# One load for both graphs of a pair, and a rewritten end, in a four-layer graph network on one core

## The chip, the cores and the metric

The kernel runs on one core of one Trainium2 chip. Such a core has TensorE (matrix products, called PE; its weight loads are listed apart as PEld), VectorE (DVE), ScalarE (ACT), GpSimd (POOL) and SyncE (SP, which here only issues transfers), and 16 DMA engines that move data between DRAM and the on-chip memories. The metric is the time of one execution on the device in microseconds. Before the change it is 1578.65 us, the median of three runs (1576.26 to 1581.45).

## The reference

There are 128 graphs of 64 nodes with 128 features each (`x`), and a weighted adjacency matrix of 64 by 64 per graph (`adj`), about a quarter of it nonzero. Four layers follow each other, each as `x = layernorm(x + layer(x, adj))`:

- Layers 0 and 1 compute a filter for every pair of nodes from its distance: Gaussians of the distance (20 in layer 0, 64 in layer 1), a matrix to 128 features, a shifted softplus, a second matrix. Layer 0 multiplies the filter by a cosine cutoff, layer 1 by the squared adjacency value. Node i then receives the sum over j of filter(i, j) times features(j), and two small matrices with a softplus between them finish the layer.
- Layer 2 is a graph convolution: elu twice after a first matrix, then two products with the normalised adjacency matrix, each after a matrix, with an elu between them.
- Layer 3 is one product with a normalised adjacency matrix, a matrix and a relu.

```python
    x = _layernorm(x + _L0_gnn_ref(x, adj, ...), axis=-1)
    x = _layernorm(x + _L1_gnn_ref(x, adj, adj, ...), axis=-1)
    x = _layernorm(x + _L2_gnn_ref(x, adj, ...), axis=-1)
    x = _layernorm(x + _L3_gnn_ref(x, adj, ...), axis=-1)
```

## The kernel before, in words

Nearly all work is in the edges of layers 0 and 1, and only the nonzero ones are computed. At the start the kernel sorts the graphs and the nodes by their numbers of edges, packs the nonzero distances, the numbers of their neighbours and their weights into lists of fixed length ("slots of edges"), and stores these lists in DRAM: `d` (distance, four bytes), `j` (neighbour, two bytes) and `w` (weight, four bytes). The length of a list, `GSLOTS`, is 948 to 1,092 in layer 0 and 1,140 to 1,260 in layer 1, and differs by set; there are eight sets of eight pairs. The packing of later sets runs beside the edge work of earlier ones, in layer 0.

The edge work goes over 128 slots: 64 pairs of graphs in layer 0, then the same 64 in layer 1. One graph of the pair lies on partitions 0 to 63 and the other on 64 to 127. The lists of a pair are copied to all partitions of their half: each row of `j` and `w`, and of `d` in layer 1, is the same list. In layer 0 a list of distances is cut into thirds, each copied to 20 rows (the last to 24), one row per Gaussian. `later_loads` (L1362 and on) issues these loads on SP's queue: `d` first, and `j` and `w` by the inner function `late`, some steps later. Before the change every load brings the rows of one graph, so that layer 1 takes six loads a slot and layer 0 ten. There are three buffers for `d` and `w` and two for `j`, so the loads of a slot are issued one to three slots ahead, once the buffer's last reader is done.

The slots are worked off two at a time, in four to six steps of some thousand edges per graph (`steps_of`). A step makes filters for its edges: `filter_in` (L1827, into PSUM `px`), two activations to `h` (exponential and logarithm), `filter_out` (L1842, `pw`), `gather` (L1856, `pg`: the neighbours' features by a product with a one-hot matrix), and `message` (L1882, DVE, product of both). `slot_sums` (L1912, L1916) adds the messages by node. ACT's `gaussians` squares and exponentiates `d`; DVE's `one_hot` (L1803) turns `j` and `w` into the weighted one-hot matrix, in place of `w`.

When a group of pairs has its sums, queues of generators follow, one small piece of each per step: `nodes` (`node_after`: the end of layers 0 and 1), `convs` (`graph_convs`: layers 2 and 3 of groups of four pairs, one queue for even and one for odd groups), and `last` for three small last groups of two, one and one pairs. `at_phase` holds a convolution back until a given step of a pair of slots. `layernorm` takes mean and variance on DVE; for groups of four pairs the root and the scaling run on GpSimd (L1460, L1461, L1466), for smaller groups on ACT and DVE. Each piece gets its PSUM from `bank`, two buffers for all of them. Results leave through `store_rows` (GpSimd, indirect) or, for the last small groups, a plain store on SP.

The order is written out: at the end `in_order` ties every instruction of an engine to the one before it on that engine, so each engine works in the order in which the program lists its instructions, and a wait holds up all that is behind it. After the last step the queues are drained in turns, one piece of each.

Of the kernel before, what the change touches and what calls it, by code (L numbers as in the profile page):

```python
# [12 lines left out]
F32 = mybir.dt.float32  # L13
# [6 lines left out]
P = 128  # L20
A = 64
# [591 lines left out]
def sparse_stack(ctx: ExitStack, tc: tile.TileContext, t: dict, out: bass.AP, flag):  # L613
# [122 lines left out]
    def dram_ap(ap, offset, dims):  # L736
        return bass.AP(tensor=ap.tensor, offset=ap.offset + offset, ap=dims)
# [118 lines left out]

    at_step = [0]

    def at_phase(k):
        while phase[0] not in (k, None):  # L860
            yield

    def steps_later(n):
        to = at_step[0] + n
        while at_step[0] < to:
            yield
# [498 lines left out]
    def later_loads(n):  # L1365


        layer, p = pair_at(n)
        s = p // 8
        size = GSLOTS[layer][s]  # L1370
        at = (p % 8) * 2 * size
        assert (layer, s) in stored, "slots are read before they are written"
        d = edge.tile([P, MAX_SLOTS], F32, tag="d", name=f"d_{n}", bufs=3)
        j = edge.tile([P, MAX_SLOTS], BF16, tag="j", name=f"j_{n}")
        w = edge.tile([P, MAX_SLOTS], F32, tag="w", name=f"w_{n}", bufs=3)

        def load(to, name, first, n):
            engine.dma_start(to, dram_ap(slots[layer, name][s], first, [[0, to.shape[0]], [1, n]]))  # L1378

        third = size // 3  # L1380
        d = d[:, 0 : size if layer else third]
        for b in range(2):
            rows, first = slice(A * b, A * (b + 1)), at + b * size
            engine = nc.sync
            if layer == 1:
                load(d[rows], "d", first, size)
            else:
                for k, end in enumerate((NG0, 2 * NG0, A)):
                    engine = nc.scalar if n == 0 and b * k == 0 else nc.sync
                    load(d[A * b + NG0 * k : A * b + end], "d", first + k * third, third)  # L1390

        def late():
            nonlocal engine
            engine = nc.sync
            for b in range(2):
                rows, first = slice(A * b, A * (b + 1)), at + b * size
                load(j[rows, 0:size], "j", first, size)
                load(w[rows, 0:size], "w", first, size)

        return (d, j, w), late  # L1400

# [19 lines left out]

    def bank(name, n=GS):
        ps = ps_n.tile([P, 512], F32, tag="n", name=name)[:, 0 : n * P]
        return ps, ps.rearrange("p (s c) -> p s c", s=n)

# [7 lines left out]
    def tiled(name, n, q):  # L1435


        tag = f"c{q % 2}" if n == GS else f"c_{q}"
        return rings[0].tile([P, n * P], F32, tag=tag, name=f"{name}_{q}", bufs=4)

# [7 lines left out]
    def layernorm(y, dst, n, name, quick=False):  # L1448

        stats = node.tile([P, GS, 6], F32, tag="st", name=f"st_{name}", bufs=4)[:, 0:n]  # L1450
        mv = node.tile([P, GS, 2], F32, tag="mv", name=f"mv_{name}", bufs=4)[:, 0:n]
        for s in range(n):
            nc.vector.bn_stats(stats[:, s, :], y[:, s, :])
            nc.vector.bn_aggr(mv[:, s, :], stats[:, s, :])  # L1454
            if s + 1 == GS // 2 < n and not quick:
                yield
        rstd = node.tile([P, GS], F32, tag="rs", name=f"rs_{name}", bufs=4)[:, 0:n]
        yield
        if n == GS:
            nc.gpsimd.tensor_scalar(rstd, mv[:, :, 1], LN_EPS, None, ALU.add)  # L1460
            nc.gpsimd.tensor_tensor(rstd, rstd, neg_half[:, 0:n], ALU.pow)  # L1461
        else:
            act(rstd, mv[:, :, 1], AF.Ln, bias=ln_eps)
            act(rstd, rstd, AF.Exp, scale=-0.5)
        for s in range(n):
            (nc.gpsimd if n == GS else nc.vector).tensor_scalar(  # L1466
                dst[:, s, :], y[:, s, :], mv[:, s, 0:1], rstd[:, s : s + 1],
                ALU.subtract, ALU.mult,
            )
        yield  # L1470
# [128 lines left out]
    def node_after(layer, q, agg):  # L1599


        w = layers[layer]
        name = f"{layer}_{q}"
        n = agg.shape[1]
        codes = node_codes.pop((layer, q))
        u, by = bank(f"u_{name}", n)
        share = by_pair(shares.pop(q)) if layer == 0 else None
        for s in range(n):
            of = agg[:, s, :]
            if n > 1:  # L1610
# [36 lines left out]
        yield from layernorm(y, xs, n, name, layer == 1)  # L1647
        if layer == 1:
            if n < GS:
                yield from graph_convs(q)  # L1650
            else:
                convs[q % 2].append(graph_convs(q))

    def elu(ps, bias, i, q, also=()):

# [40 lines left out]

        act(to, ps, AF.Copy)

    normals = {}

    def normals_of(q):

# [9 lines left out]
    def graph_convs(q):  # L1712
# [14 lines left out]
            return y  # L1727

        if n == GS:
            yield from at_phase(6)  # L1730
            scaled(2, q)
        flat, ps = bank(f"gx_{q}", n)
        for s in range(n):
# [17 lines left out]
        yield True  # L1751
        nT3 = by_pair(tiled("nTs3", n, q)) if n == GS else normals[3, q]
        h1 = yield from elu(flat, g["b1"], 1, q, normal(3, q, nT3) if n == GS else ())
        y2 = yield from times("hw2", lambda s: h1[:, s, :], lambda s: g["W2"])
        _, ps = bank(f"o2_{q}", n)
        for s in range(n):
# [4 lines left out]
        yield  # L1761
        yield from layernorm(z, xs, n, f"2_{q}")
        if n == GS:
            yield from at_phase(2)
        y3 = yield from times("sup", lambda s: xs[:, s, :], lambda s: nT3[:, s, :])
        flat, ps = bank(f"o3_{q}", n)
        nc.tensor.matmul(
# [153 lines left out]
            else:  # L1921
                nodes.append(node_after(layer, q, agg))

    befores, nodes, convs, sums = deque(), deque(), (deque(), deque()), deque()
    small_groups, small = range(NP // GS - 1, len(GROUPS[1])), {}
    at_end = range(NP // GS - 2, len(GROUPS[1]))
    last = {q: deque() for q in small_groups}
# [122 lines left out]
    for i in range(len(steps) + 2):  # L2050
# [29 lines left out]
        if c is not None:  # L2080
# [4 lines left out]
            for part_ in c["parts"]:  # L2085
# [25 lines left out]
        if layer == 0:  # L2111
            slot(nodes)
            if befores and phase[0] in BEFORES[beat]:
                slot(befores)
        if c2 is not None:
            filter_out(c2)
        for queue in last.values():
# [2 lines left out]
            slot(nodes)  # L2120
        if c2 is not None:
            message(c2)
        for _ in range(1 + (n >= N - MORE)):
            if convs[0]:
                slot(convs[0])
# [5 lines left out]
        for _ in range(1 + (n >= N - MORE)):  # L2131
            slot(convs[1])
        for queue in last.values():
            slot(queue)
        past = [c, c1]
    phase[0] = None
    run(sums, -1)
# [52 lines left out]
```

## Time and profile before

| | |
|---|---|
| median of three runs | 1578.65 us |
| profiled execution | 1577.26 us |
| its span | 1575.4 us |
| PE busy | 1427.4 us, 91% |
| DVE, ACT busy | 1316.5 us (84%), 1313.8 us (83%) |
| POOL busy | 759.3 us, 48% |
| mean DMA rate over the span | 131 GB/s |
| first and last `filter_in` of layer 0 | 67.6 and 725.2 us |
| first and last `filter_in` of layer 1 | 729.2 and 1494.7 us |
| last `one_hot` | 1481.7 us |

The profile is one execution taken by the hardware profiler; times in it count from the start of its span. A busy share is an average over the whole run and says little by itself: the stages have different limits, so the table of busy time by stage is read first, then the chain of waits (from the last instruction back, at each step to what released it), then the DMA queues, where a packet is one contiguous piece moved by one DMA engine, and a completion is a further packet of four bytes. A label such as L1842 is a line of the kernel before; L955 is a helper through which all activations go. The names left and right of an arrow are what an instruction writes and reads.

### The profile page before, as it was taken

The page shows a single profiled execution, that of the slowest core. Times are in us where ns is not written, and L with a number is a line of the kernel's source. Part 1 is how long each engine was busy: PE and PEld are TensorE (multiplying, and loading weights), DVE is VectorE, ACT ScalarE, POOL GpSimd, SP SyncE. Part 2 cuts the span into 40 slices and gives each one's busy share as a digit, 9 for nine tenths or more (in the row PEclk, how much of TensorE's full clock was granted, in tenths as well). Part 3 has the DMA queues.
Part 4 walks back from the last instruction along what each step waited for, and adds up shares of the span by engine and source line. Part 5 has one row for each costly group of instructions (what it writes and reads, how often), then busy time and mean ns, then how long its engine had stood idle before and what let it go on. Part 6 is the DMA issues. An engine that isn't in the chain of part 4 may idle for free.

```text
span 1575.4 us, 23201 instructions
## 1 busy us (share of the span) xinstructions
PE 1427.4 (91%) x6841; PEld 790.8 (50%) x6841; DVE 1316.5 (84%) x2895; ACT 1313.8 (83%) x1647; POOL 759.3 (48%) x1175
## 2 busy tenths in 40 slices
PE   1387999999989999999999999999999999998974
PEld 1143454554444445554444555555555655554553
DVE  8796988888989899788788888888888888878763
ACT  1366897989888989899999999999999999988742
POOL 2435256365564545333912334555544665555544
PEclk9999999999999999999999999999999999999985
DMA  6766454545555545447665655555555555654100
GB/s 205 258 139 137 101 136 116 129 123 136 130 142 124 141 130 135 125 114 167 155 152 142 143 132 132 147 133 136 139 130 138 139 132 131 150 132 106 31 7 23
DMA packets 122280, 205.60 MB, mean 131 GB/s; under 512 B 47956, under 2 KB 80034, under 8 KB 121506
## 3 DMA queue, kind: packets, MB, share of 16 engines
q1 hardware_dynamic: 113330, 188.40, 48.2%
q0 software_dynamic: 6576, 14.99, 2.9%
q8 instruction: 57, 0.93, 0.3%
q10 hardware_dynamic: 2240, 0.65, 0.2%
q14 instruction: 77, 0.63, 0.1%
HBM read 185.29 MB, written 18.64 MB: 129 GB/s over the span
## 4 chain that ended last, share of the span: by engine, by line
PE 61%; ACT 11%; DVE 9%; DMA 6%; issue 4%; SPq 2%; POOL 2%; another core or an unknown queue 1%; DVEq 0%; ACTq 0%; POOLq 0%
PE pw L1842 23%; PE px L1827 13%; PE pg L1856 11%; ACT h L955 5%; DVE m L1882 2%; DMA w<-w_dram 2%; DVE agg L1912 2%; DMA j<-j_dram 2%; ACT d L955 2%; PE y L1491 1%; PE hw L1722 1%; SPq L1378 1%; PE u L1615 1%; PE back L1641 1%; PE o L1632 1%
## 5 line engine op out<-in xcount | busy, mean ns | idle before, releaser
L955 ACT ACTIVATE h<-h,half 128x1008 f32<-128x1008 f32 (+12 forms) x313 | 332.8, 1063 | 0.1
L955 ACT ACTIVATE m<-pg 128x1008 f32<-128x1008 f32 (+12 forms) x313 | 291.8, 933 | 46.1 <-DVE agg L1916 21.0
L1856 PE MATMUL pg<-w,ys 64*128 64x504 f32 (+15 forms) x1376 | 299.4, 518 | 27.0 <-ACT d L955 7.5
L1842 PE MATMUL pw<-h,w_L_gnn_W2T 128*128 128x504 f32 (+8 forms) x640 | 300.2, 592 | 2.6 <-DVE m L1882 2.4
L1882 DVE SCALAR_TENSOR_TENSOR m<-pw,c_L_gnn_b,m 128x1008 f32<-128x1008 f32 (+8 forms) x161 | 194.8, 1211 | 113.6 <-PE pw L1842 97.7
L1912 DVE TENSOR_REDUCE agg<-m 128x32 f32<-128x544 f32 (+14 forms) x455 | 287.2, 669 | 1.8 <-PE u L1615 0.4
L1842 PE MATMUL pw<-h,w_L_gnn_fw 128*128 128x504 f32 (+6 forms) x608 | 253.6, 540 | 9.7 <-DVE m L1882 7.7
L1882 DVE SCALAR_TENSOR_TENSOR m<-pw,c_L_gnn_fb,m 128x1008 f32<-128x1008 f32 (+6 forms) x152 | 168.8, 1111 | 69.9 <-PE pw L1842 47.2
L955 ACT ACTIVATE h<-px,c_L_gnn_b 128x1008 f32<-128x1008 f32 (+8 forms) x160 | 171.4, 1071 | 30.2 <-PE px L1827 30.0
L955 ACT ACTIVATE h<-px,c_L_gnn_fb 128x1008 f32<-128x1008 f32 (+6 forms) x152 | 148.2, 975 | 53.8 <-PE px L1827 37.9
L1856 PEld LDWEIGHTS pg<-w,ys 64*128 64x128 f32 x1376 | 129.0, 189 | 118.6 <-issue 50.3
L1842 PEld LDWEIGHTS pw<-h,w_L_gnn_W2T 128*128 128x128 f32 x640 | 109.4, 191 | 153.5 <-issue 82.0
L1803 DVE SCALAR_TENSOR_TENSOR w<-j,row,w 128x1212 f32<-128x1212 bf16 (+12 forms) x128 | 181.3, 1416 | 5.4 <-DMA w<-w_dram 5.4
L1827 PE MATMUL px<-d,fw 64*128 64x168 f32 (+10 forms) x928 | 155.4, 440 | 27.1 <-DMA d<-d_dram 18.4
L1827 PE MATMUL px<-d,w1t 64*128 64x504 f32 (+11 forms) x768 | 173.1, 542 | 0.5 <-ACT h L955 0.4
L1460 POOL TENSOR_SCALAR rs<-mv 128x4 f32<-128x4 f32 x61 | 15.0, 245 | 288.7 <-DVE mv L1454 288.0
L1842 PEld LDWEIGHTS pw<-h,w_L_gnn_fw 128*128 128x128 f32 x608 | 105.3, 193 | 90.9 <-issue 44.9
L1827 PEld LDWEIGHTS px<-d,fw 64*128 64x128 f32 x928 | 74.4, 189 | 127.8 <-issue 36.1
L955 ACT ACTIVATE d<-d,neg_off 128x1212 f32<-128x1212 f32 (+12 forms) x128 | 120.9, 945 | 8.2 <-DMA d<-d_dram 8.2
L995 POOL DMA_INDIRECT rows<-comb,goes x64 | 71.0, 1110 | 108.9 <-DMA rows<-comb,goes 64.5
L1466 POOL TENSOR_SCALAR x_all<-ny,mv,rs 128x128 f32<-128x128 f32 x124 | 109.2, 889 | 3.3
L995 POOL DMA_INDIRECT out_dram<-gz,at_row x56 | 75.1, 1341 | 60.1 <-DMA out_dram<-gz,at_row 55.0
(264 smaller groups left out, 2300.8 us busy)
## 6 DMA issues: line engine op xcount, KB each, us to landing
d<-d_dram SPq DMA_DIRECT2D x32, 315.0 KB
w<-w_dram SPq DMA_DIRECT2D x32, 315.0 KB
d<-d_dram SPq DMA_DIRECT2D x32, 303.0 KB
w<-w_dram SPq DMA_DIRECT2D x32, 303.0 KB
w<-w_dram SPq DMA_DIRECT2D x32, 252.0 KB
j<-j_dram SPq DMA_DIRECT2D x32, 157.5 KB
j<-j_dram SPq DMA_DIRECT2D x32, 151.5 KB
d<-d_dram SPq DMA_DIRECT2D x16, 300.0 KB
```

Of the source, the lines that this page charges most:

```text
L955: latest = nc.scalar.activation(out_, in_, func, **kw)
L995: nc.gpsimd.indirect_dma_start(out=into, out_offset=bass.IndirectOffsetOnAxis(ap=at, axis=0), in_=rows, in_offset=None,)
L1378: engine.dma_start(to, dram_ap(slots[layer, name][s], first, [[0, to.shape[0]], [1, n]]))
L1466: (nc.gpsimd if n == GS else nc.vector).tensor_scalar(dst[:, s, :], y[:, s, :], mv[:, s, 0:1], rstd[:, s : s + 1], ALU.subtract, ALU.mult,)
L1491: nc.tensor.matmul(ps[:, s, :], lhsT=xt[:, s * P : (s + 1) * P], rhs=w["win"], start=True, stop=True)
L1615: nc.tensor.matmul(by[:, s, :], lhsT=w["o1"], rhs=of, start=layer == 1, stop=True)
L1803: nc.vector.scalar_tensor_tensor(hots[n][:, 0:size], j[:, 0:size], near, wt[:, 0:size], ALU.is_equal, ALU.mult)
L1827: nc.tensor.matmul(ps[:, b, at : at + m], lhsT=w["w1"][rows, :] if c["layer"] else w["w1"][rows, k, :], rhs=d[rows, col : col + m], start= ...
L1842: nc.tensor.matmul(c["pw"][:, b, :], lhsT=c["w"]["w2"], rhs=c["h"][:, b, :], start=True, stop=True)
L1856: nc.tensor.matmul(ps[:, b, to], lhsT=y[rows, :], rhs=hots[part_["n"]][rows, first:stop], start=True, stop=True,)
L1882: nc.vector.scalar_tensor_tensor(to, c["pw"][:, :, of], c["w"]["b2"], to, ALU.add, ALU.mult)
L1912: nc.vector.tensor_reduce(av[:, :, :, r], both, AX.X, ALU.add)
```

## The change

Three things are changed.

The first is `later_loads`. One load now brings the rows of both graphs of a pair: the destination is all 128 partitions, and the source is read as [2][64][size], the first step going from one graph's list to the other's, the second repeating a list 64 times. In layer 0 two of the three thirds of one graph are brought by one load, [2][20][third].

```diff
-        def load(to, name, first, n):
-            engine.dma_start(to, dram_ap(slots[layer, name][s], first, [[0, to.shape[0]], [1, n]]))
+        both = [[size, 2], [0, A], [1, size]]
+
+        def load(to, name, first, dims):
+            engine.dma_start(to, dram_ap(slots[layer, name][s], first, dims))
...
-        for b in range(2):
-            rows, first = slice(A * b, A * (b + 1)), at + b * size
-            engine = nc.sync
-            if layer == 1:
-                load(d[rows], "d", first, size)
-            else:
-                for k, end in enumerate((NG0, 2 * NG0, A)):
-                    engine = nc.scalar if n == 0 and b * k == 0 else nc.sync
-                    load(d[A * b + NG0 * k : A * b + end], "d", first + k * third, third)
+        engine = nc.sync
+        if layer == 1:
+            load(d, "d", at, both)
+        else:
+            for b in range(2):
+                first = at + b * size
+                load(d[A * b : A * b + 2 * NG0], "d", first, [[third, 2], [0, NG0], [1, third]])
+                engine = nc.scalar if n == 0 and b == 0 else nc.sync
+                load(
+                    d[A * b + 2 * NG0 : A * (b + 1)], "d", first + 2 * third,
+                    [[0, A - 2 * NG0], [1, third]],
+                )
+                engine = nc.sync
 
         def late():
...
-            for b in range(2):
-                rows, first = slice(A * b, A * (b + 1)), at + b * size
-                load(j[rows, 0:size], "j", first, size)
-                load(w[rows, 0:size], "w", first, size)
+            load(j[:, 0:size], "j", at, both)
+            load(w[:, 0:size], "w", at, both)
```

The second is the end after the last step. Six queues (`x`, `y`, `z` for the small groups, `a`, `b`, `c` for the convolutions) get a PSUM bank of their own each, cut out of the banks of the edge work, and a written string says whose turn is next; a turn goes on until its queue has issued something.

```diff
     def bank(name, n=GS):
+        if own_banks:
+            ps = own_banks[now_run[0]][:, 0 : n * P]
+            return ps, ps.rearrange("p (s c) -> p s c", s=n)
...
-    while nodes or convs[0] or convs[1] or any(last.values()) or stores:
-        for queue in (*last.values(), nodes, *convs):
-            slot(queue)
+    run(nodes, -1)
+    for pool, tag, keys in ((ps_x, "x", "zy"), (ps_g, "g", "ab"), (ps_w, "w", "xc")):
+        both = pool.tile([P, 2, 512], F32, tag=tag, name=f"own_{tag}")
+        for h, key in enumerate(keys):
+            own_banks[key] = both[:, h, :]
+    queues = dict(zip("xyz", last.values()), n=nodes, a=convs[0], b=convs[1], c=convs[2])
+    turns = 'cbzyxybazyxzybcbcbaxyycybbczxyczxaxzyczxzxabxyczcbzyxcbybazxbxyczzcbzczycxyyyzyczcbyxczxzzbxxyzxzycbczcyxczcyyxzyzyzbxxyxzbzxczxzxzzcyyxczzyz'
+    while any(queues.values()):
+        for key in turns:
+            now_run[0], size = key, len(block)
+            while queues[key] and len(block) == size:
+                run(queues[key], 1)
+            run(stores, 1)
+        turns = "zyxcba"
```

The third is what leads up to it. After the last step, and for the three norms of the last group of four pairs (`LAST`, group 14), root and scaling run on ACT and DVE. This group gets a third convolution queue and tiles of its own; the small groups' normalised matrices (`normals_of`) are begun 14, 11 and 8 slots before the end; convolutions are free of their phase in the last four slots instead of eight, and wait one or two steps there; the sums of the last pair are shared out differently.

```diff
-        if n == GS:
+        apart = n == GS and not own_banks and name not in own_names
+        if apart:
             nc.gpsimd.tensor_scalar(rstd, mv[:, :, 1], LN_EPS, None, ALU.add)
             nc.gpsimd.tensor_tensor(rstd, rstd, neg_half[:, 0:n], ALU.pow)
...
-            (nc.gpsimd if n == GS else nc.vector).tensor_scalar(
+            (nc.gpsimd if apart else nc.vector).tensor_scalar(
...
-    def at_phase(k):
+    def at_phase(k, later=0):
+        if phase[0] is None and not own_banks:
+            yield from steps_later(later)
         while phase[0] not in (k, None):
             yield
...
-                convs[q % 2].append(graph_convs(q))
+                convs[2 if q == LAST else q % 2].append(graph_convs(q))
...
-            yield from at_phase(6)
+            while q == LAST and (3, q - 2) not in turned:
+                yield
+            yield from at_phase(6, 1)
...
-    FREE, MORE = 8, 0
+    FREE, MORE, ONCE, FAST = 4, 4, 1, (0, 0)
+    SUMS = (2, 2, 3, 4, 4)
+    EARLY = {N - gap: q for gap, q in zip((14, 11, 8), small_groups)}
...
-        if n >= N - 4:
-            run(sums, (2, 2, 5, 4, 2)[k] if c is not None else 9)
+        if n >= N - 2:
+            run(sums, SUMS[k] if c is not None else 9)
...
-                if layer == 1 and part_["s"] == 0 and q in last:
-                    last[q].append(normals_of(q))
+                if m in EARLY:
+                    last[EARLY[m]].append(normals_of(EARLY[m]))
```

More of the change, by code (lines that the diff above doesn't have):

```diff
@@ L1375, in later_loads @@
         w = edge.tile([P, MAX_SLOTS], F32, tag="w", name=f"w_{n}", bufs=3)
-        def load(to, name, first, n):
-            engine.dma_start(to, dram_ap(slots[layer, name][s], first, [[0, to.shape[0]], [1, n]]))
+        both = [[size, 2], [0, A], [1, size]]
+        def load(to, name, first, dims):
+            engine.dma_start(to, dram_ap(slots[layer, name][s], first, dims))
         third = size // 3
         d = d[:, 0 : size if layer else third]
-        for b in range(2):
-            rows, first = slice(A * b, A * (b + 1)), at + b * size
-            engine = nc.sync
-            if layer == 1:
-                load(d[rows], "d", first, size)
-            else:
-                for k, end in enumerate((NG0, 2 * NG0, A)):
-                    engine = nc.scalar if n == 0 and b * k == 0 else nc.sync
-                    load(d[A * b + NG0 * k : A * b + end], "d", first + k * third, third)
-        def late():
-            nonlocal engine
-            engine = nc.sync
-            for b in range(2):
-                rows, first = slice(A * b, A * (b + 1)), at + b * size
-                load(j[rows, 0:size], "j", first, size)
-                load(w[rows, 0:size], "w", first, size)
+        engine = nc.sync
[11 more added lines that the diff above has]
+                engine = nc.sync
+        def late():
+            load(j[:, 0:size], "j", at, both)
+            load(w[:, 0:size], "w", at, both)
         return (d, j, w), late
@@ L1420, in sparse_stack @@
     g["W3"] = load_matrix("L3_gnn_WT")
+    own_banks, now_run = {}, [None]
+    own_names = [f"{i}_{NP // GS - 2}" for i in (1, 2, 3)]
     def bank(name, n=GS):
+        if own_banks:
+            ps = own_banks[now_run[0]][:, 0 : n * P]
+            return ps, ps.rearrange("p (s c) -> p s c", s=n)
         ps = ps_n.tile([P, 512], F32, tag="n", name=name)[:, 0 : n * P]
@@ L1435, in tiled @@
     def tiled(name, n, q):
+        if q == LAST:
+            tag = dict(
+                gxt="na", nTs2="nh", em0="agg", er0="bk", gy_hw1="na", nTs3="agg",
+                em1="bk", er1="na", gy_hw2="bk", gz2="na", gy_sup="nh", gz3="bk",
+            )[name]
+            return node.tile([P, GS * P], F32, tag=tag, name=f"{name}_{q}", bufs=1)
         tag = f"c{q % 2}" if n == GS else f"c_{q}"
@@ L1697, in copy @@
         act(to, ps, AF.Copy)
-    normals = {}
+    normals, turned = {}, set()
     def normals_of(q):
@@ L1753, in graph_convs @@
         h1 = yield from elu(flat, g["b1"], 1, q, normal(3, q, nT3) if n == GS else ())
+        turned.add((3, q))
         y2 = yield from times("hw2", lambda s: h1[:, s, :], lambda s: g["W2"])
@@ L1763, in graph_convs @@
         if n == GS:
-            yield from at_phase(2)
+            yield from at_phase(2, 2)
         y3 = yield from times("sup", lambda s: xs[:, s, :], lambda s: nT3[:, s, :])
@@ L1922, in slot_sums @@
                 nodes.append(node_after(layer, q, agg))
-    befores, nodes, convs, sums = deque(), deque(), (deque(), deque()), deque()
+    befores, nodes, convs, sums = deque(), deque(), (deque(), deque(), deque()), deque()
+    LAST = NP // GS - 2
     small_groups, small = range(NP // GS - 1, len(GROUPS[1])), {}
@@ L2114, in sparse_stack @@
                 slot(befores)
+        if n >= N - MORE:
+            slot(nodes)
+            if not ONCE:
+                slot(convs[2])
+        if N - FAST[0] <= n < N - FAST[1]:
+            slot(convs[1])
         if c2 is not None:
@@ L2122, in sparse_stack @@
             message(c2)
-        for _ in range(1 + (n >= N - MORE)):
-            if convs[0]:
-                slot(convs[0])
+        if convs[0]:
+            slot(convs[0])
+        if n >= N - MORE:
+            slot(convs[2])
         if c is not None and turn["gauss"] is not None:
@@ L2130, in sparse_stack @@
                 begun[m] = stage + 1
-        for _ in range(1 + (n >= N - MORE)):
-            slot(convs[1])
+        slot(convs[1])
         for queue in last.values():
@@ L2136, in sparse_stack @@
     phase[0] = None
+    if owing is not None:
+        run(owing, 1)
+        owing = None
     run(sums, -1)
-    while nodes or convs[0] or convs[1] or any(last.values()) or stores:
-        for queue in (*last.values(), nodes, *convs):
-            slot(queue)
+    run(nodes, -1)
[4 more added lines that the diff above has]
+    queues = dict(zip("xyz", last.values()), n=nodes, a=convs[0], b=convs[1], c=convs[2])
+    at_end_of_steps = None
+    turns = 'cbzyxybazyxzybcbcbaxyycybbczxyczxaxzyczxzxabxyczcbzyxcbybazxbxyczzcbzczycxyyyzyczcbyxczxzzbxxyzxzycbczcyxczcyyxzyzyzbxxyxzbzxczxzxzzcyyxczzyz'
[6 more added lines that the diff above has]
+        turns = "zyxcba"
+    while stores:
         run(stores, 1)
```

## The prediction

> **What bounds the kernel now.** I read the stages, then the chain of waits, then the DMA views. Busy time by stage (after the stretch: its length, then busy us and count of PE, PEld, DVE, ACT, POOL, then granted PE clock, DMA share, GB/s), for the edge work of layer 0, of layer 1, and the end:
>
> ```profile
> 64.00:725.00 661.00, 610.99 (x2969) 323.28 (x2971) 574.84 (x1491) 559.90 (x738) 317.81 (x515) 0.98 0.53 131
> 729.00:1495.00 766.00, 752.84 (x3611) 422.49 (x3612) 642.44 (x1060) 713.12 (x822) 387.82 (x426) 1.00 0.53 132
> 1495.00:1575.00 80.00, 48.74 (x206) 34.30 (x202) 43.16 (x141) 27.15 (x72) 36.16 (x48) 0.72 0.05 15
> ```
>
> TensorE holds the edge work (611 of 661 us, 753 of 766); the 16 DMA engines are 53% busy. A layer has 64 slots (a slot is one pair): 661/64 = 10.3 us a slot, then 766/64 = 12.0. The last 80 us are short dependent steps. In layer 0 the chain of waits (start, length, what) does pass through loads:
>
> ```profile
> 207.19 5.54 DMA w<-w_dram
> 212.72 0.02 issue
> 212.74 1.94 DMA d<-d_dram
> ```
>
> Some 18 such places of 1.5 to 5.5 us lie on it, 60 us together. Now the queues, and two windows that hold one slot's d loads and no other transfer, 157.3 to 160.7 us (layer 0) and 1448 to 1452 us (layer 1):
>
> ```profile
> q1 hardware_dynamic: 113330, 188.40, 48.2%
> q10 hardware_dynamic: 2240, 0.65, 0.2%
> ```
> ```profile
> DMA packets 192, 0.19 MB, mean 55 GB/s; under 512 B 64, under 2 KB 192, under 8 KB 192
> ```
> ```profile
> DMA packets 160, 0.65 MB, mean 161 GB/s; under 512 B 32, under 2 KB 32, under 8 KB 160
> ```
>
> Layer 1: two loads of 64 rows are 128 data packets and 32 small ones, 16 completions a load, one from each DMA engine it used. Layer 0: six loads (four of 20 rows, two of 24) are 128 data packets and 64 small ones, not 96; 64 = 4x10 + 2x12. **A load is spread over the largest number of engines, up to 16, that divides its rows.** Which side's rows, q10 (ScalarE's queue) tells. By the program its transfers move 1,981 data packets; the page has 2,240, so 259 completions. Six blocks of 20 rows give 60; slot 0's d (20+20+20+24) 42; nine transfers of 64 or 128 rows 144; a single row 1: 247. The 12 left fall to four loads whose destination has 60 rows and whose source reads [3][20][1]: 3 each, not the 15 that 60 alone would allow. So the number must divide the outermost dimension of the source too. The same rule over every transfer of q1 gives 19,877 completions; its records hold 20,901 packets of 4 bytes, of which 1,024 are data: exact.
>
> What one engine moves, from the window 3 to 9 us, where large loads keep all 16 busy (GB/s in 40 slices):
>
> ```profile
> GB/s 382 382 355 437 328 382 355 437 382 410 437 328 410 410 437 410 437 355 437 437 416 396 447 369 399 430 396 447 430 304 324 270 292 288 290 273 289 268 270 268
> ```
>
> The first 29 slices mean 403, most often 410 and 437: I take 410/16 = 25.6 GB/s an engine. The fastest tenth of the 5,040-byte packets agrees (194 ns, 26.0 GB/s).
>
> **The change part by part.** *Loads.* d of layer 1 and every j and w become one load with destination 128 rows and source [2][64][size]; d of layer 0 becomes, per graph, one load of 40 rows from [2][20][size/3] and one of 24. SP issues 448 fewer DMAs (6 to 3 per slot in layer 1, 10 to 6 in layer 0), at about 0.6 us each on SP, of which only those in front of a wait on the chain count. But the outermost source dimension is now 2, so by the rule **each of these loads runs on two engines.** Which two: in layer 0's 10- and 12-engine loads the records show 10 to 12 packets in flight for 10.7 us and 13 or more for 0.45 us, while 64-row loads hold 16 for 66 us. Loads that took turns round the 16 engines would pass 12 freely; so a load of fewer engines starts at the same engine each time, and all merged loads share one pair.
>
> Bytes for one engine of that pair, with sizes from the kernel's table: a layer-1 slot of size s brings 64 rows of d (4s bytes), w (4s) and j (2s), 640s bytes; the eight sizes sum to 9,612, times 8 slots: 49.2 MB. A layer-0 slot brings 64 rows of w and j (384s) and 40+4 rows of d of 4s/3 bytes (58.7s); sizes sum to 8,196: 29.0 MB. 78.2 MB at 25.6 GB/s is **3,055 us**: 30 us a slot in layer 1 against 12.0 of compute, 17.7 in layer 0 against 10.3. So the cover is gone: one-hot (L1803 before) waits for w at each slot, DVE holds messages and sums behind it, ACT's Square and Exp wait for d, and PE for both. With three buffers of d and w and two of j, the next slot's loads are queued while one lands, so the pair of engines stays fed. PE may fall to a lower clock in the pauses: at the 0.72 of the end row, 10.3 and 12.0 become 14 and 17 us, still under the loads.
>
> Bounds of the rate: quickest 447/16 = 27.9 GB/s (2,803 us); slowest the mean of q1 under contention, 188.40 MB in 48.2% of 16x1575.4 us = 15.5 GB/s (5,045 us). I take 25.6, since two engines do not crowd each other as 16 do.
>
> *Other traffic on the pair.* q0 takes 2.9% of the span on every engine (46 us); the rest of q1 after the start (28 MB less some 14 in the first 60 us, over 16 engines, 0.9 MB) 35 us: 80 us.
>
> *Gaps.* SP waits in order for buffers and for round trips of the sorting in layer 0; where its queue runs dry the pair idles. Between 0 and 6.8 us a slot (the 2.2 us issue of a d load and a landing of 4.6, as the chain has them, every time: 870 us). I take the 60 us that loads hold on the chain now, since one slot's loads are always queued ahead.
>
> *Start and end.* The first d load issues at 63 us, unchanged. From the last one-hot (1481.7) to the end of the execution (1577.26; span 1575.4) are 95 us. End edits: norms of four pairs leave GpSimd after the last step. One costs there 0.23 + 1.04 + 4x0.79 and gaps, 4.7 us; with ACT's Ln and Exp (0.29 + 0.20) and four DVE scalings (0.4 each) 2.4. The chain's last 60 us hold 11 us of it and 7 us of waits for row stores (`out_dram<-gz`) that stood on the same engine in front of a norm; half of the first and all of the second go: 12.6. DVE is 26 of those 60 us busy and ACT 19, so the work fits. Six PSUM banks in place of two: PE's bank waits there sum to under 2 us; 0 to -2, taken -1. Later release of the graph convolutions (four slots in place of eight, one or two steps more), earlier small normals, other sums and the written list order the same instructions anew, and three norms of the last group of four leave GpSimd inside the edge work, where DVE and ACT wait for loads: between +10 (a late group) and -20 (the idle of PE), taken 0. End: 95 - 14 = 81.
>
> Sum: 63 + 3,055 + 80 + 60 + 81 = 3,339, made against the profiled 1577.26, 1.4 under the median of the runs: **3,340 us, 2.1 times the time before.** Within 0.3% (4.7 us) is no measurable change.
>
> [...]
>
> **The rivals.** (1) *Faster: the load runs on 16 engines.* Then two issues of 0.6 us fall away at each of the 18 places (-22), and the end gives -14: 1,541. For it: the bytes are the same. Against it: the 3 completions of the [3][20][1] source. It decides from five engines on: a layer-1 slot's 1.54 MB in 12.0 us needs 128 GB/s, five times 25.6. (2) *Two engines, but another pair each time.* A w load then takes 12.6 us but loads overlap, and they are issued one to two slots ahead (10 to 24 us); perhaps a third of layer 0's slots wait 5 us: +105, less 14: 1,668. Against it: the packets in flight. (3) *One pair at the contended rate:* 5,045 + 284 = 5,330. Against it: two engines read two different rows.
>
> **How the numbers follow.** Forecast 0.84; (1) 0.06; (2) 0.05; (3) 0.05. The forecast's own ends: 2,803 with no gaps, 3,027; and 3,055 with 4.5 us of gap a slot, 3,855. The transfers may run a little above the best slice, so 2,850 to 3,900, which holds most of the forecast's 0.84. Case (1) is faster (0.05), or within 0.3% if its gains do not come (0.01); all else is slower.
>
> **What would show it.** d, j and w loads of some 600 KB landing 12 us and more after issue; DMA share falling from 0.53 to about 0.16 (two engines of 16 full, the others at 3%) while the loads are the wait on the chain; 2 completions a load, so q1's packets fall by about 11,900 (14,336 completions of these loads become 2,432); PE busy under half; slots of about 18 and 30 us; the wait of one-hot on w at the head of the list. It is wrong if the records show 16 completions a load, or two engines with different pairs. The end is right if POOL's norms are gone after the last step and the stretch after the last one-hot is 75 to 90 us.

## The result and the profile after

The changed kernel takes 3390.9 us, the median of four runs (3390.5 to 3391.7), against 1578.8 us of the kernel before on the same chip: a ratio of 2.148, with a 95% interval of 2.144 to 2.152. The prediction was 3,340 us. The profiled execution took 3391.66 us, its span 3389.9.

Busy time by stage, with the columns of the table shown of before: edge work of layer 0, of layer 1, and the stretch from the last one-hot to the end.

```profile
71.00:1402.00 1331.00, 768.13 (x2971) 405.61 (x2971) 571.17 (x1487) 558.37 (x736) 285.29 (x510) 0.76 0.20 63
1419.00:3306.80 1887.80, 954.07 (x3536) 496.61 (x3536) 628.10 (x1025) 713.17 (x808) 341.84 (x410) 0.72 0.14 55
3306.80:3389.90 83.10, 54.76 (x277) 41.13 (x278) 61.32 (x189) 36.97 (x97) 18.86 (x24) 0.81 0.05 15
```

No engine fills its stage any more: PE is busy 768 of 1,331 us and 954 of 1,888, and works at a granted clock of 0.72 to 0.76. The count of its instructions is the same; the work is there, it waits. Two stages grew; the third, 93.7 us before by the same marks (1481.7 to 1575.4 us), did not.

The chain of waits by engine and by line, and 46 us of it in layer 1 (start, length, what):

```profile
DMA 83%; SPq 5%; PE 3%; ACT 3%; DVE 2%; issue 1%; POOL 0%; DVEq 0%; ACTq 0%
DMA d<-d_dram 54%; DMA w<-w_dram 29%; SPq L1382 4%; ACT d L957 1%; PE pw L1862 1%; ACT h L957 1%; PE pg L1876 1%; DMA x_all<-x_sorted 1%; PE px L1847 1%; DVE w L1823 0%; DVE m L1902 0%; ACT m L957 0%; SPq L1610 0%; DVE st L1469 0%; DVE agg L1932 0%
```
```profile
2392.61 9.92 SPq L1382
...
2402.62 33.03 DMA d<-d_dram
2435.66 0.02 issue
2435.68 1.27 ACT d L957
```

Where `filter_out` held 35% of such a stretch before (1300 to 1345 us), the chain now goes from load to load. A load of `d` is on it for 33 us: the `j` and `w` that SP issued just before it, at 2380 and 2391 us, stand in front of it. On two engines each load is 64 rows an engine; at this run's means for these sizes, 96 ns for a row of `j` and 183 for one of `w` or `d`, the three are 6.1, 11.7 and 11.7 us, 29.5 of the 33. Then the waits (engine and line, what it waited for: us in total, times, longest), and the queues (packets, MB, share of 16 engines):

```profile
ACT d L957 <- DMA d<-d_dram: 1784.5, 122, 23.2
DVE w L1823 <- DMA w<-w_dram: 960.0, 126, 21.4
PE pg L1876 <- DVE w L1823: 644.4, 94, 14.5
```
```profile
q1 hardware_dynamic: 101516, 188.44, 15.4%
q10 hardware_dynamic: 2150, 0.56, 0.1%
```

ACT's Square waits for `d` and the one-hot for `w` at practically every slot. The same megabytes went through q1, in 15.4% of the engines' time instead of 48.2% of a span less than half as long. Five microseconds in layer 1 (2400 to 2405 us) show how: 53 GB/s, and 12.8% of 16 engines, which is two of them full.

```profile
DMA packets 60, 0.26 MB, mean 53 GB/s; under 512 B 1, under 2 KB 1, under 8 KB 60
q1 hardware_dynamic: 60, 0.26, 12.8%
```

Counted over the records of layer 1, exactly two large packets are in flight for 1,791 of 1,904 us, and none for 4.7 us.

### The profile page after: what moved, and what is told of

Same layout as the page of the kernel before. It is cut to its first block, busy times and chain, and to the rows that moved or that the text cites. A ratio compares the mean times of both kernels' runs of the same rounds, so it can differ in the third digit from the quotient of the medians.

```text
span 3389.9 us, 22342 instructions
## 1 busy us (share of the span) xinstructions
PE 1793.8 (53%) x6840; PEld 955.2 (28%) x6841; DVE 1323.7 (39%) x2919; ACT 1324.1 (39%) x1659; POOL 674.1 (20%) x1139
## 3 DMA queue, kind: packets, MB, share of 16 engines
q1 hardware_dynamic: 101516, 188.44, 15.4%
## 4 chain that ended last, share of the span: by engine, by line
DMA 83%; SPq 5%; PE 3%; ACT 3%; DVE 2%; issue 1%; POOL 0%; DVEq 0%; ACTq 0%
DMA d<-d_dram 54%; DMA w<-w_dram 29%; SPq L1382 4%; ACT d L957 1%; PE pw L1862 1%; ACT h L957 1%; PE pg L1876 1%; DMA x_all<-x_sorted 1%; PE px L1847 1%; DVE w L1823 0%; DVE m L1902 0%; ACT m L957 0%; SPq L1610 0%; DVE st L1469 0%; DVE agg L1932 0%
## 5 line engine op out<-in xcount | busy, mean ns | idle before, releaser
L1876 PE MATMUL pg<-w,ys 64*128 64x504 f32 (+15 forms) x1376 | 416.3, 689 | 652.6 <-DVE w L1823 644.4
L1847 PE MATMUL px<-d,w1t 64*128 64x504 f32 (+11 forms) x768 | 229.7, 696 | 433.8 <-ACT h L957 433.8
L1876 PEld LDWEIGHTS pg<-w,ys 64*128 64x128 f32 x1376 | 160.6, 244 | 797.3 <-issue 624.7
L1862 PE MATMUL pw<-h,w_L_gnn_W2T 128*128 128x504 f32 (+8 forms) x640 | 352.3, 679 | 4.7 <-DVE m L1902 4.4
L1862 PE MATMUL pw<-h,w_L_gnn_fw 128*128 128x504 f32 (+6 forms) x608 | 296.1, 617 | 3.7 <-DVE m L1902 3.2
L1847 PEld LDWEIGHTS px<-d,w1t 64*128 64x128 f32 x768 | 73.9, 227 | 486.9 <-ACT h L957 454.3
L1847 PE MATMUL px<-d,fw 64*128 64x168 f32 (+10 forms) x928 | 162.2, 454 | 54.6 <-ACT h L957 27.6
L1862 PEld LDWEIGHTS pw<-h,w_L_gnn_W2T 128*128 128x128 f32 x640 | 131.1, 228 | 209.9 <-issue 157.1
L1862 PEld LDWEIGHTS pw<-h,w_L_gnn_fw 128*128 128x128 f32 x608 | 127.4, 233 | 107.1 <-issue 66.2
L1777 PE MATMUL o<-gy_hw,nTs 128*128 128x128 f32 x104 | 24.9, 416 | 191.2 <-ACT gy_hw L957 191.2
```

Source lines behind the costliest of these rows:

```text
L1777: nc.tensor.matmul(ps[:, s, :], lhsT=nT[:, s, :], rhs=y2[:, s, :], start=True, stop=True)
L1847: nc.tensor.matmul(ps[:, b, at : at + m], lhsT=w["w1"][rows, :] if c["layer"] else w["w1"][rows, k, :], rhs=d[rows, col : col + m], start= ...
L1862: nc.tensor.matmul(c["pw"][:, b, :], lhsT=c["w"]["w2"], rhs=c["h"][:, b, :], start=True, stop=True)
L1876: nc.tensor.matmul(ps[:, b, to], lhsT=y[rows, :], rhs=hots[part_["n"]][rows, first:stop], start=True, stop=True,)
```

## The experiments

Every ratio below is against the kernel before, run on the same chip in the same batch. "Theory" is that of the prediction: a load occupies the largest number of engines, up to 16, that divides the outermost dimension of both sides, always the same ones, and these are the bound.

**Which part of the change does it.** The first run is the kernel after with the loads of before, those of `d` in layer 0 too:

```diff
-            load(d, "d", at, both)
+            for b in range(2):
+                load(d[A * b : A * (b + 1)], "d", at + b * size, [[0, A], [1, size]])
...
-            load(j[:, 0:size], "j", at, both)
-            load(w[:, 0:size], "w", at, both)
+            for b in range(2):
+                load(j[rows, 0:size], "j", first, size)
+                load(w[rows, 0:size], "w", first, size)
```

> The kernel after with the loads of the kernel before (one graph each). Theory (all of the loss is in the loads, the end gains the 14 us of the prediction): 1,563 us. Rival A (the end edits gain nothing once the loads are whole): 1,577. Rival B (part of the loss is in the end or in the later release of the convolutions): above 1,580.

It took 1560.7 us, ratio 0.9885 (0.9868 to 0.9901): faster than both kernels, than the one before by 1%. The second run is the other half, the kernel before with `load`, `both` and `late` of the kernel after:

```diff
-                load(d[rows], "d", first, size)
+            load(d, "d", at, both)
...
+            load(j[:, 0:size], "j", at, both)
+            load(w[:, 0:size], "w", at, both)
```

> The kernel before with the merged loads alone. Theory: all of the loss, and the end's 14 us not gained: 3,405 us, two packets in flight for most of the span. Rival A: 3,391, the end is worth nothing behind such loads. Rival B: clearly under 3,300, if the two parts of the change cost more together than alone.

It took 3405.8 us, ratio 2.158 (2.153 to 2.162). So the loads alone make the whole loss. The end edits gain 18 us with the loads of before, and some 15 us with merged loads, by the ratios 2.158 and 2.148.

**Is it the source's shape, or that both graphs come in one load?** In the kernel before every load keeps its one graph, its 64 rows and its number of issues; only the source is written as two nested repetitions of the same list, [k][64/k][size] in place of [64][size], with k of 2, 4 and 8:

```diff
-            engine.dma_start(to, dram_ap(slots[layer, name][s], first, [[0, to.shape[0]], [1, n]]))
+            over = [[0, k], [0, to.shape[0] // k]] if to.shape[0] == A else [[0, to.shape[0]]]
+            engine.dma_start(to, dram_ap(slots[layer, name][s], first, [*over, [1, n]]))
```

> The kernel before, no load merged, but in every load of 64 rows the repeat of the list is written [2][32][size] instead of [64][size]: the same bytes by the same number of loads. Theory (the outermost dimension of the source sets the number of engines, always the same ones): two engines carry all of j and w and layer 1's d; layer 0's d stays on 10 and 12 engines, which takes 32 rows of 53 ns a slot off the pair, 64 x 1.7 = 109 us: about 3,290. Rival A (merging two graphs in one load is what costs): 1,579. Rival B (loads of two engines take another pair each time): 1,600 to 1,700.

> As the run before, with [4][16][size]: four engines. Theory: in layer 1 an engine moves 2 x 16 rows of d, w and j, 14.9 us a slot against 12.0 of compute; in layer 0 8.0 and 2.5 of other traffic, 10.5 against 10.3. 63 + 725 + 954 + 90 = about 1,830. Rival A: 1,579. Rival B: 1,579 to 1,620.

> The kernel before with every list repeated as [8][8][size]: eight engines a load. Theory of throughput alone: an engine needs 7.5 us a slot in layer 1 and some 6.5 in layer 0, both under the compute: 1,579 to 1,600. Rival (the landing time of a load counts too, since in layer 0 loads are issued hardly a slot ahead; four engines lost 270 us there where throughput alone gave 64): layer 0 loses some 60 to 100 us, layer 1 nothing, 1,640 to 1,680.

They took 3499.7 us (ratio 2.217, 2.213 to 2.221), 2068.2 us (1.310, 1.306 to 1.314) and 1682.9 us (1.064, 1.061 to 1.068). The line of q1 in each, k of 2, 4 and 8:

```profile
q1 hardware_dynamic: 104370, 188.36, 15.5%
```
```profile
q1 hardware_dynamic: 105650, 188.37, 28.0%
```
```profile
q1 hardware_dynamic: 108210, 188.38, 40.4%
```

640 loads have 64 rows. If each sends k completions in place of 16, the 113,330 packets of before fall by 640 x 14, 12 and 8, to 104,370, 105,650 and 108,210: exact to the packet. With bytes, rows, issues and buffers unchanged, an outer dimension of 2 in the source alone more than doubled the time (2.217).

What an engine then does in layer 1 can be added up: the 24,576 rows that layer 1 brings are divided among the engines of a load, and each row has its measured time. The last column is layer 1 from its first packet to its last landing.

| engines per load | mean of a row of `d` or `w`, of `j` | rows an engine carries, `d` and `w` + `j` | its sum | layer 1 took |
|---|---|---|---|---|
| 2, kernel after | 186.5 ns, 98.1 ns | 8,192 + 4,096 | 1,930 us | 1,904 us |
| 2, k = 2 | 187.2, 97.9 | 8,192 + 4,096 | 1,935 us | 1,908 us |
| 4, k = 4 | 189.1, 99.3 | 4,096 + 2,048 | 978 us | 980 us |
| 8, k = 8 | 263.8, 133.8 | 2,048 + 1,024 | 677 us | 808 us |
| 16, kernel before | 303.3, 157.2 | 1,024 + 512 | 391 us | 750 us |

With two and four engines the layer lasts as long as those engines are busy, within 1.5%. Two misses stand beside that. With k = 4, layer 0 took 933 us against 725 expected: in 254 of them no row of `j` or `w` is in flight, and these gaps add themselves to the engines' work, where I had let them run beside it. With k = 2 the run took 210 us more than the 3,290 expected: its layer 0 took 92 us longer than in the kernel after, where I had expected it 109 us shorter, because the rows of `d` leave the pair. Over all slots of layer 0 a row of `w` took 183 ns in place of 162 and a row of `j` 103 in place of 93, which with 4,096 rows of each an engine makes 87 and 43 us; and for 159 us no row was in flight, in place of 93. Together that makes up for what the rows of `d` save and adds about 60 of the 92 us. Why rows and pauses are longer there only, with the separate loads of layer 0, stays open.

With k = 8 nothing is full by that sum, and yet 6% are lost. The rival of that run came nearest, 3 us above its range, but not by its account: it had layer 1 lose nothing, and against the kernel before layer 0 grew by 55 us and layer 1 by 58. The chain by line shows where:

```profile
PE pw L1843 15%; DMA out_dram<-gz,at_row 14%; PE px L1828 9%; PE pg L1857 7%; DMA w<-w_dram 4%; DMA d<-d_dram 3%; DMA rows<-comb,goes 3%; SPq L1379 2%; ACT h L955 2%; POOL x_all L1467 2%; PE u L1616 1%; DVE m L1883 1%; DMA rows<-rows 1%; PE gh L1751 1%; DVE agg L1913 1%
```

GpSimd's row stores are 14% of it, and they are not among the lines that the page names for the chain of before. Their waits in the kernel before, with k = 8, and in the run of `j` below, with those of ACT's Square for `d` in the last two (8.2 us before):

```profile
POOL out_dram L995 <- DMA out_dram<-gz,at_row: 55.0, 28, 3.0
```
```profile
POOL out_dram L995 <- DMA out_dram<-gz,at_row: 94.8, 34, 5.2
ACT d L955 <- DMA d<-d_dram: 87.8, 38, 9.2
```
```profile
POOL out_dram L995 <- DMA out_dram<-gz,at_row: 142.0, 38, 6.6
ACT d L955 <- DMA d<-d_dram: 250.1, 68, 12.3
```

The packet records show why. A row store of GpSimd is 16 pieces of 4,096 bytes on another queue, q0. Of the 44 row stores that each run makes first, all beside the loads of layer 1, I counted the pieces that start more than 1 us after the first piece of their store. In the kernel before there are none for 40 stores, and the last piece starts 0.6 us after the first in the median. With one or all kinds of load on two engines there are exactly two in nearly every store (43 of 44 in the kernel after, 44 with k = 2 and in the run of `w` below, 41 in the run of `j`), with k = 4 four in all 44, and with k = 8 eight in 30. The median from first to last is 2.7 us in the kernel after, 3.2 with k = 8 and 4.0 in the run of `j`. I read this as the pieces on a busy engine waiting and the others not; what GpSimd has to do behind the store waits with it (94.8 and 142.0 us in the two runs shown above, 55.0 before). This also counts the confined engines a second time, from another queue's packets.

**One kind of load at a time.** In the kernel before only `w`, or only `j`, is merged ([2][64][size]); all else keeps 16 (or 10 and 12) engines. The diff is that for `w`; for `j` the same lines carry `j`.

```diff
+        both = [[size, 2], [0, A], [1, size]]
+
+        def load_both(to, name):
+            engine.dma_start(to, dram_ap(slots[layer, name][s], at, both))
...
+            load_both(w[:, 0:size], "w")
...
-                load(w[rows, 0:size], "w", first, size)
```

> The kernel before with w alone merged, j and d as before. Theory: only w is confined to two engines, 10.2 us a slot in layer 0 and 12.0 in layer 1, and with the pair's share of the other loads 13.3 and 14.2 us, against 10.3 and 12.0 of compute: 63 + 853 + 911 + 81 and up to 100 of gaps, 1,910 to 2,010. Rival (landing time in layer 0 as in the run before): 2,050 to 2,150. If merging does not matter in itself: 1,579.

> The kernel before with j alone merged. Theory: j's 64 half-long rows take one engine 5.3 us a slot in layer 0 and 6.1 in layer 1, with its share of the rest some 9 us, under the compute in both layers: 1,579 to 1,600. Rival (landing time): the one-hot of a slot waits for j, which lands some 5 us later than now, and layer 0 shows it: 1,640 to 1,750.

They took 2270.1 us (ratio 1.435, 1.432 to 1.439) and 1905.2 us (1.205, 1.201 to 1.208). Both lie above all that was expected, the rivals too. For `w` such a sum accounts for layer 1. The DMA share (tenths of 16 engines) and GB/s over 20 us of layer 1, 1400 to 1420 us, in 40 slices:

```profile
DMA  7999211778400111111031011011013799971386
GB/s 218 349 233 271 49 55 58 107 233 247 102 39 39 58 58 48 48 58 58 39 91 58 39 58 58 39 58 58 39 58 87 247 325 204 281 175 34 73 218 199
```

Bursts at a DMA share of 0.7 and more alternate with long stretches at about 0.1, which is two engines of 16, and 39 to 58 GB/s, in which the pair alone works off `w`. In layer 1 each engine of the pair carries 4,096 rows of `w`, 512 of `d` and 512 of `j`. At 188 ns for a row of `w`, the price of a row that runs undisturbed (187 to 189 with two and four engines in the table), the mean of `d` and `w` together, 249 ns, leaves 309 for `d`; `j` has 136. That makes 770 + 158 + 70 = 998 of the 1,047 us that the layer took. The pair is thus 95% full, if the rows of `w` did run undisturbed, which their records cannot tell from those of `d`. The expectation had priced all of it at 25.6 GB/s, 911 us: by the same split the rows of `d` in the crowded bursts cost 1.6 times that. Layer 0 took 1,060 us, of which 245 pass with no row of `j` or `w` in flight: its gaps add themselves to the pair's work instead of running beside it.

For `j` alone, the rows of one engine of the pair fill 712 of layer 1's 879 us (4,096 rows of `j` at their mean of 127 ns and 1,024 of `d` and `w` at 187, the undisturbed price), or 854 with the mean of `d` and `w` in this run, 325 ns. No row at all is in flight for 84 us, 10%. The pair is thus 81 to 90% busy, `w` lands late behind the 64 rows of `j` (8.1 us at 127 ns), and the row stores behind both: 24% and 16% of this run's chain are the waits for `w` and for row stores. How much each of the two costs was not separated.

**The end, part by part.** Each of three runs takes the first run (1560.7 us) and undoes one edit; a fourth puts one edit alone into the kernel before. The other edits (the third convolution queue, the earlier small normals, the later release, the sums) were not run one by one.

```diff
-        apart = n == GS and not own_banks and name not in own_names
+        apart = n == GS
```

> The end-only kernel (loads of one graph, 1,560.7 us) with the norms of four pairs back on GpSimd. Theory (the norms and the row stores they stand behind are 12.6 of the end's gain): about 1,573. Rival (the written list and the banks bring it): 1,561 to 1,564.

With the norms back on GpSimd: 1574.3 us, ratio 0.9957 (0.9942 to 0.9971).

```diff
-    turns = 'cbzyxybazyx ...'
+    turns = "zyxcba"
```

> The end-only kernel with the written list replaced by plain turns, z y x c b a over and over. Theory (the list was taken at 0): 1,561. Rival (the order is worth up to 20 us): 1,565 to 1,580.

With plain turns in place of the written list: 1575.6 us, ratio 0.9965 (0.9950 to 0.9981).

```diff
-        if own_banks:
+        if None in own_banks:
```

> The end-only kernel, but every queue takes its PSUM from the two shared buffers of before, the list kept. Theory (banks are worth 1 us): 1,562. Rival (with six queues interleaved by the list the two buffers stall TensorE): 1,570 and more.

With the two shared PSUM buffers, the list as it is: 1569.4 us, ratio 0.9923 (0.9907 to 0.9939).

```diff
-        if n == GS:
+        apart = n == GS and not ended
+        if apart:
...
+    ended.append(True)
```

> The kernel before with one thing changed: after the last step the norms of four pairs run on ACT and DVE. Theory: 1,578.7 less 12.6, about 1,566. Rival (without the new order the chain only moves to DVE): 1,573 to 1,579.

With only the norms after the last step taken off GpSimd, the kernel before gives 1573.2 us, ratio 0.9938 (0.9919 to 0.9957).

Against the first run's 0.9885 the norms are worth 0.7%, the list 0.8%, the banks 0.4%, some 11, 13 and 6 us. Each of these differences is uncertain by some 4 us. Their sum is more than the 18 us of all edits together, so they are not separate gains. The norms alone bring 0.6%, 10 us, about what undoing them costs; so the overlap should lie between the list and the banks. That a list written for six banks is worth less with two is my reading of it, and no run has the list or the banks alone. What the norms do can be read from one group of instructions, on GpSimd in the kernel before (L1466) and on DVE in the first run (L1481); it is (count, shortest, median, longest in ns, first and last start):

```profile
L1466 POOL TENSOR_SCALAR gz<-gz,mv,rs x12: 787/792/803, 1503.0 to 1565.9; 128x128 f32<-128x128 f32 x12
```
```profile
L1481 DVE TENSOR_SCALAR gz<-gz,mv,rs x16: 314/340/346, 1525.5 to 1554.3; 128x128 f32<-128x128 f32 x16
```

And the chain of the three runs that undo an edit names what came back. From 1475 us on, GpSimd has 21 us of it with the norms on it, waits for row stores 9 us with plain turns, and the first run has neither; products have 41 us with shared banks against 33 in the first run. Two pieces of each, in that order (start, length, what):

```profile
1522.08 3.12 POOL gz L1481 x4
1527.11 3.13 POOL x_all L1481 x4
```
```profile
1524.82 2.47 DMA out_dram<-gz,at_row
1528.06 2.37 DMA out_dram<-gz,at_row
```
```profile
1515.19 2.09 PE hw L1737 x8
1550.83 2.09 PE sup L1737 x8
```

## Why the prediction was right, and where not

*The step on which all hung, two engines, always the same pair.* Right, and shown: 9,027 packets of four bytes in q1, which is the 20,901 of before less the 11,874 completions by which the rule lets q1 fall; two packets in flight; two late pieces in a row store; the same loss from a source of [2][32] with nothing else changed. It was read from three completions of a load of another shape in the profile of before. That the engines are always the same pair follows from the count in flight with several loads queued (two, not four or six). A queue that took one load after the other would show two as well, but it did not work so: in layer 1 of the run of `j`, two rows of `j` are in flight for 414 us, and in 181 of them five or more rows of `d` and `w` of the same queue run beside them. Which two engines they are, no record shows. One count of the argument was off: the 66 us with "16" packets of 64-row loads in flight hold 15 as well, and 16 alone makes 41 us; the argument rests on the 0.45 us and stands.

*The price of a byte, 25.6 GB/s an engine.* Right for long rows: those of 5,040 bytes took 194 ns in the median (26.0 GB/s), the fastest tenth of before. Shorter rows cost more a byte here: in layer 0 the means are 162 ns for `w`, 93 for `j` and 72 for `d`, which is 25.4, 22.0 and 19.0 GB/s. The other end of the range, the crowded 15.5 GB/s of rival (3), did not occur: a row of `d` or `w` of layer 1 takes 187 ns with two engines and 303 with 16.

*The sum by stages.* Layer 1, from 1,402 us to the last landing at 3,306, took 1,904 us; 49.2 MB at 25.6 GB/s are 1,922. Layer 0 took 1,339 us, against 1,133 of bytes, 80 of other traffic and 60 of gaps, 1,273. The end took 85 us against 81. The misses, -18, +66 and +4, are the 52 us by which the profiled 3391.7 lies above the sum. Layer 0 is the stage that was mis-sized, in two terms. No row of `d`, `j` or `w` was in flight for 92.8 us, where I had taken the 60 us of waits on the chain of before: +33. And an engine of the pair carries there 4,096 rows of `w`, 4,096 of `j` and 2,816 of `d`, which at the means above, delays by other traffic included, make 1,246 us against the 1,133 of bytes and 80 of other traffic: +33 again (the mean of `d` is that of all its rows). For 110 us of it only one row was in flight. The argument that one slot's loads are always queued ahead held in layer 1 (4.7 us with nothing in flight) and not in layer 0. There SP, whose queue also carries the loads and stores of the sorting, waits 34 times for a `w` to land before it issues its next load, against 24 short waits before (first line before, second after: us in total, times, longest):

```profile
SPq L1378 <- DMA w<-w_dram: 16.8, 24, 1.7
SPq L1382 <- DMA w<-w_dram: 220.8, 34, 9.9
```

That the misses of the three stages partly cancel is luck.

*The end.* The sum came out near for reasons that were half right. Norms were predicted at 12.6 us and measured at 10 alone and 11 in place. The list was taken as 0 and is worth some 13 us in place, the banks as 1 and are worth 6: the end edits gain 18 us, not 14. Not all of it lies behind the last one-hot: that stretch shrinks from 95 to 85 us in the kernel after and to 86 in the first run, where the last one-hot also starts 4.5 us earlier. POOL's norms are gone after the last step, as said; one still runs at 3311 us, during the last steps.

*The signs.* Slots of 20.7 and 29.7 us (18 and 30 predicted), DMA share 0.20 and 0.14 in the two layers (0.16), and the load of `d` shown above landed 33 us after its issue (12 and more). Two were missed slightly: PE was busy 53%, not under half, its instructions taking longer, at the granted clock of 0.72 to 0.76 (1793.8 us for 6,840 of them, in place of 1427.4 for 6,841); and the one-hot's wait for `w` stands second, behind ACT's wait for `d`, which is issued ahead of `j` and `w` of its own slot but behind those of the slot before.

*The rivals.* (1) fell with the completions, and its threshold fell with the k runs: "it decides from five engines on" compared megabytes with an uncrowded price. Eight engines could move 205 GB/s by that price against 128 needed, and the run with them lost 6.4%; a row took 264 ns, not 187, and GpSimd's waits for row stores grew from 55.0 to 94.8 us. (2) fell with two packets in flight, (3) with the price of a row.

## What to carry to other kernels

Before merging two transfers, write down the outermost dimension of both sides: if merging puts a 2 there, count two engines, as the runs here showed (2 completions a load, two packets in flight), divide the bytes by two, and compare that time with the stage's compute, slot by slot. Here the number of completion packets told it from a profile before any run: three for the [3][20][1] source. Loads on two engines here also came with late pieces of another queue's transfers (2.7 us from the first to the last piece of a row store, 0.6 before), so "enough GB/s on average" is not yet hidden; and a change that bundles a large loss with small gains is worth taking apart, as the first experiment gave the best kernel here, 1560.7 us.

## What the runs showed of the hardware that was not expected

A row took less time with two and four engines a load than with eight, and less with eight than with 16: the mean for `d` and `w` of layer 1 was 187, 189, 264 and 303 ns. From two to four engines the sum of an engine's rows fell by half (1,930 to 978 us); from four to eight, and from eight to 16, by less (to 677 and 391).

In the kernel after, two of the 16 pieces of a row store, on another queue, came late: 2.7 us from the first to the last piece in the median, the time of some 14 rows at 187 ns.

With all loads on the pair, SP's queue was also held while it issued them. The issuing instruction of `w` on SP's queue, before and after (count, then shortest, median and longest in ns, first and last start):

```profile
L1378 SPq DMA_DIRECT2D w<-w_dram x256: 3/587/1357, 65.0 to 1457.4; - x128
```
```profile
L1382 SPq DMA_DIRECT2D w<-w_dram x128: 512/7169/15912, 66.6 to 3268.5; - x128
```

Issuing half as many loads was to save SP about 0.6 us each; instead one issue took 7.2 us in the median and up to 15.9. With k = 8 it was 0.57 us again, and 0.54 with `w` alone on the pair. In layer 1 it can have cost little, as the pair was full in any case (4.7 of 1,904 us without a row in flight); in layer 0 the loads and stores of the sorting stand behind it on that queue, and what that cost was not measured by itself. The granted clock of TensorE was lower in runs in which PE was busy for less of the span: 0.98 before with 91%, 0.96 with k = 8 (87%), 0.89 with k = 4 (76%), 0.75 after (53%).
